# Two stores of layer 2 on ScalarE's DMA queue, and 16 buffers for the count blocks of the early products

## The chip, the cores and the metric

The kernel runs on one core of a Trainium2 chip. The metric is the device time of one execution, in microseconds (us); the time of a kernel is the median of several executions. A core has TensorE (PE), VectorE (DVE), ScalarE (ACT), GpSimd (POOL) and SyncE (SP). Each engine executes its own instructions in order, and SP, ACT and POOL each have a queue through which they issue DMA transfers. An instruction that waits for something holds all that is behind it on the same engine, DMA issues too.

## The reference

A graph network on 6250 nodes and 100,000 edges (sorted by destination): layer norm and ReLU, four SAGE layers of width 256 to 512, a final dense layer and a residual. Cut to what matters:

```
deg = segment_sum(ones, dst)
h1 = sage_mean(h0)                                   # 256 -> 512
hp = relu(h1 @ W2_pool + b2_pool)                    # layer 2: max pooling
hmax = where(deg > 0, segment_max(hp[src], dst), 0)
h2 = h1 @ W2_self + hmax @ W2_neigh + b2
h3 = ((segment_sum(h2[src], dst) + h2) / (deg + 1)) @ W3_neigh + b3
h4 = sage_mean(h3)
out = x + h4 @ W_fc + b_fc
```

The kernel merges weights across the layers: the products with `W3_neigh`, `W4_*` and `W_fc` are folded into the weights of layer 2, so that layer 2 gives rows that layer 3 only sums over the edges.

## The kernel before

**Tiles.** Nodes are cut into 49 tiles of 128, sorted edges into 782 tiles of 128. A sum over edges has two forms. For the destination tiles with many edges (0 to 15 for layer 3) it is a matrix product with a **count matrix** A: for each destination tile 49 blocks of 128 x 128 counts in fp8, made in the kernel and kept in DRAM as `tab_a` (784 KB for each of 18 tiles). For the others the source rows are gathered edge by edge. Rows that are summed later are kept to full precision as three bf16 parts (hi, mid, lo).

**Order of the work.** Layer 2 is one loop over the 782 edge tiles, in blocks and written out by hand; on each turn it advances several side works by a step each: the count matrices still to be made (`hub`), the early products (`early`) and the generators of finished node tiles (`now`). A scheduler then orders the instructions of each engine. In the profiled execution layer 2 lies at about 895 to 2330 us, its max pooling with what the change touches at about 1070 to 2330.

**The row flow.** Line L1354 (POOL) gathers 128 rows of 512 float32 values (256 KB) into X, which holds two such tiles; there are six X buffers (three each in two pools). L1335 (DVE) takes a running maximum over edges of one destination. L1339 (`stored`, SP) writes the rows to DRAM (`rows`). An X buffer is free for the next gather when DVE has read it and its store has landed. At the end of a block `carry` (L1197 to L1229) mends the first rows.

**done2 (L1243 on), once for each of the 49 node tiles.** `totals` gathers the maxima of the tile (L1235, POOL) and loads the first layer's tile th (L1241, through ACT's queue). PE transposes the maxima (L1254), ACT copies them (L1257), PE multiplies in float32 (L1261, L1264, L1267). Then the result is split: ACT casts hi (L1275), PE subtracts it (L1277), ACT casts mid (L1279), PE subtracts it (L1281), ACT casts lo (L1283), and **L1284 stores the three parts** `r3` (384 KB) to `tab_r`, through SP. Layer 3 reads `tab_r`.

**build_narrow (L356 on), for count matrices of the tiles 8 to 17.** ACT (L365, L372) and DVE (L367) make one-hot matrices, PE counts (L383), ACT copies the counts into A (L388), L398 checks them, and **L392 stores the finished matrix**, through SP. The tiles 0 to 7 are stored at L348, in another function, through SP as well.

**The early products.** While layer 2 still runs, the products of layer 3 for the count tiles 0 to 15 begin: as soon as four new row tiles are split (row tiles 37 down to 6), `early_products` adds 16 pieces of work. Each loads four count blocks (64 KB, L1311, SP) into a buffer `ae` (**L1310**), PE multiplies (L557, in `dense`), and the sum goes into `acc3` (L1125 on DVE, the first time L1128 on ACT). There are 128 such loads. The class `Hub` calls the load of a piece `LOOK` = 4 pieces ahead of its product, and `ae` has `LOOK + 3` = 7 buffers.

The parts of the code that the change touches:

Of the kernel before, what the change touches and what calls it, by code (L numbers as in the profile page):

```python
# [10 lines left out]
BF16 = mybir.dt.bfloat16  # L11
F16 = mybir.dt.float16
F8 = mybir.dt.float8e4
# [7 lines left out]
P = 128  # L21
# [57 lines left out]
def fast_path(  # L79
# [15 lines left out]
    nc = tc.nc  # L95
# [69 lines left out]
    tab_r = dram.tile([NP, 3 * FH], BF16, name="tab_r")  # L165
    tab_s = dram.tile([NP, 3 * FO], BF16, name="tab_s")
    tab_a = dram.tile([H4, P, NT, P // 2], BF16, name="tab_a")
# [79 lines left out]
    def bank(pool, tag, name, shape=None, bufs=None):  # L247
        t = pool.tile([P, FH], F32, tag=one_tag.get(id(pool), tag), name=name, **({"bufs": bufs} if bufs else {}))
        if shape is None:
            return t  # L250
        n = math.prod(shape)
        if len(shape) == 1:
            return t[:, :n]
        return t[:, :n].rearrange("p (a b) -> p a b", b=shape[1])
# [98 lines left out]
    def build_narrow(d, keys, pool, psb, copies):  # L353

        sk, mk, r0 = keys
        work = []  # L356
        held = {}
        for v in range(WT2):
            r = row_of[NW1 + (d - H1) * WT2 + v, 0] - r0

            def hot(r=r, v=v):
                i = v % 4
                if i == 0:
                    held["ht"] = pool.tile([P, 4, P], BF16, name="ht", bufs=2)
                nc.scalar.activation(held["ht"][:, i, :], iota_b, AF.Abs, bias=sk[:, r : r + 1])  # L365
                hm = pool.tile([P, NT * WIN2], BF16, name="hm", bufs=16)
                nc.vector.tensor_scalar(hm, iota_w[:, : NT * WIN2], mk[:, r : r + 1], None,  # L367
                                        op0=ALU.is_equal)
                held["hm", v] = hm
                if i == 3:  # L370
                    hs = pool.tile([P, 4, P], BF16, name="hs", bufs=5)
                    nc.scalar.activation(hs, held["ht"], AF.Relu, bias=one, scale=-1.0)  # L372
                    held["hs", v // 4] = hs

            def run(v=v):
                if v == 0:
                    held["A"] = pool.tile([P, NT, P], F8, name="A", bufs=2)
                A = held["A"]
                i = v % 2
                if i == 0:  # L380
                    held["pb"] = bank(psb, "pb", "pb", (2 * NT, WIN2))
                pb = held["pb"]
                nc.tensor.matmul(pb[:, i * NT : (i + 1) * NT, :].rearrange("p s c -> p (s c)"),  # L383
                                 held["hs", v // 4][:, v % 4, :], held.pop(("hm", v)),
                                 start=True, stop=True)
                def copy(pb=pb):
                    c = (v - 1) * WIN2
                    nc.scalar.copy(  # L388
                        A[:, :, c : c + 2 * WIN2].rearrange("p s (i c) -> p i s c", c=WIN2),
                        pb.rearrange("p (i s) c -> p i s c", s=NT), saturate=True)  # L390
                    if v == WT2 - 1:
                        nc.sync.dma_start(tab_a[d], A.bitcast(BF16))  # L392

                def look(n):
                    s0, s1 = LOOKS[n]
                    at = NW1 + len(LOOKS) * (d - H1) + n
                    many = pool.tile([P, 13, P], BF16, name="many", bufs=1)
                    nc.scalar.activation(many[:, : s1 - s0, :], A[:, s0:s1, :], AF.Relu,  # L398
                                         bias=less, accum_out=most[:, at : at + 1])

                if i == 1:
                    for f in copies[:2]:
                        f()
                    del copies[:2]
                    copies.insert(0, copy)
                    if v == WT2 - 1:
                        copies.extend(lambda n=n: look(n) for n in range(len(LOOKS)))

            work.append((hot, run))
        return work  # L410

    LOOK = 4
# [555 lines left out]
    with ExitStack() as on:  # L968
# [9 lines left out]
        def done1(d, acc):  # L978
# [31 lines left out]
            for k in range(KI):  # L1010
# [11 lines left out]
                        lambda acc, d=d: todo.append(done1(d, acc)), extra=3)  # L1022
# [107 lines left out]
    with tc.tile_pool(name="fl2c", bufs=1) as ck, ExitStack() as late:  # L1130
# [113 lines left out]
        def done2(d):  # L1244
            tots, th = totals(d)
            for _ in range(6):
                yield
            hm = tots[0]
            for t in tots[1:]:
                nc.vector.tensor_tensor(hm, hm, t, op=ALU.max)  # L1250
            yield
            pt = bank(pst, "pt", "pt_hTf", (KH, P))
            for j in range(KH):
                nc.tensor.transpose(pt[:, j, :], hm[:, j * P : (j + 1) * P], ident)  # L1254
            yield
            hT = wk.tile([P, KH, P], F32, name="hTf")
            nc.scalar.copy(hT, pt)  # L1257
            yield
            pm = bank(psm, "pm", "pm_prf")
            for k in range(KI):  # L1260
                nc.tensor.matmul(pm, th[:, k, :], usA[:, k, :], start=(k == 0), stop=False)  # L1261
            yield
            for k in range(KI):
                nc.tensor.matmul(pm, th[:, KI + k, :], usB[:, k, :], start=False, stop=False)  # L1264
            yield
            for c in range(KH):
                nc.tensor.matmul(pm, hT[:, c, :], un[:, c, :], start=False, stop=(c == KH - 1))  # L1267
                if c == 1:
                    yield
            yield  # L1270
            yield
            yield
            r3 = early_pool[0].tile([P, 3 * FH], BF16, name="r3", bufs=2 * BATCH + 1)
            hi, mid, lo = (r3[:, i * FH : (i + 1) * FH] for i in range(3))
            nc.scalar.copy(hi, pm)  # L1275
            yield
            nc.tensor.matmul(pm, minus_b, hi, start=False, stop=True, skip_group_check=True)  # L1277
            yield
            nc.scalar.copy(mid, pm)  # L1279
            yield  # L1280
            nc.tensor.matmul(pm, minus_b, mid, start=False, stop=True, skip_group_check=True)  # L1281
            yield
            nc.scalar.copy(lo, pm)  # L1283
            nc.sync.dma_start(tab_r[d * P : (d + 1) * P, :], r3)  # L1284
            if EARLY[0] <= d < EARLY[1]:
                ready.append((d, r3))
                if len(ready) == BATCH or d == EARLY[0]:
                    early_products()
            yield


        BATCH = 4
        ready = []
        early = Hub()
        early_pool = []
        summed = []

        def take_sums():
            while summed:
                add3(*summed.pop(0))  # L1300

        def early_products():
            batch = dict(ready)
            ss = sorted(batch)
            ready.clear()
            for d in range(H3):
                got = {}

                def load(d=d, got=got):
                    got[0] = early_pool[0].tile([P, BATCH, P], F8, name="ae", bufs=LOOK + 3)  # L1310
                    nc.sync.dma_start(got[0][:, : len(ss), :].bitcast(BF16),  # L1311
                                      tab_a[d, :, ss[0] : ss[-1] + 1, :])

                work = dense(ss, lambda s, got=got: got[0][:, s - ss[0], :],
                             lambda s: batch[s], FH, psd, lambda v, d=d: summed.append((d, v)),
                             own=d)

                def then(w):
                    take_sums()
                    w()  # L1320

                early.add([(load, work[0])] + [lambda w=w, i=i: then(w) if i == len(work) - 2 else w()
                                               for i, w in enumerate(work[1:])])
# [22 lines left out]
        for b in reversed(range(NB)):  # L1346
# [3 lines left out]
            for s0 in range(0, tb, G2):  # L1350
                X = (xmore if at // G2 % 2 else xpool).tile([P, G2, FH], F32, name="X2")
                for k in range(G2):
# [40 lines left out]
                    if (tiles and not ends and at >= begun_at + 11  # L1393
                            and begun2 < NT * (at - FIRST_AT) / (T - 20 - FIRST_AT)):
                        begun_at = at
                        now.append(done2(tiles.pop(0)))
                        begun2 += 1
# [10 lines left out]
        while tiles or now:  # L1408
            if tiles and len(now) < 2:
                now.append(done2(tiles.pop(0)))  # L1410
            for g in list(now):
                if next(g, 0) == 0:
                    now.remove(g)
# [42 lines left out]
    with ExitStack() as on:  # L1456
# [11 lines left out]
        with tc.tile_pool(name="fl3", bufs=2) as wk:  # L1468
# [36 lines left out]
            for d in range(H3):  # L1505
                work += dense([s for s0, s1 in late for s in range(s0, s1)], lambda s, d=d: block(d, s), lambda s: Z3[s], FH, psd,
                              lambda acc, d=d: todo.append(done3(d, acc)), own=d)
# [3 lines left out]
        with tc.tile_pool(name="fl4", bufs=2) as wk:  # L1511
# [22 lines left out]
            for d in range(H4):  # L1534
                parts4.append(dense([s for s0, s1 in order for s in range(s0, s1)],
                                    lambda s, d=d: block(d, s), lambda s: Z4[s], FO, psd,
                                    lambda acc, d=d: todo.append(done4(d, acc)), wide=True))
# [652 lines left out]
```

## Time and profile before

| | |
|---|---|
| time, median of 3 runs | 3315.81 us (3312.7 to 3325.22) |
| profiled execution | 3345.5 us, its span 3343.4 us |
| granted TensorE clock, mean | 0.895 of full speed |
| busy in the span | PE 75%, DVE 62%, POOL 58%, ACT 28% |
| DMA | 806.43 MB, mean 241 GB/s |
| DMAs of layer 2 through SP | 384 KB to `tab_r` x49; 256 KB rows; 64 KB `ae` x128; `tab_a` x18 (10 of them L392) |

The page of a profile shows one execution. A group of instructions has a name such as "L1284 SPq DMA_DIRECT2D tab_r<-r": the line of the kernel, the engine (SPq is SP's DMA queue, ACTq is ScalarE's), the operation, and what it writes and reads. A line of the waits, "SPq L1284 <- ACT r L1283: 141.4, 21, 16.9", says that the engine stood idle ahead of L1284 for 141.4 us in total, 21 times and at most 16.9 us, until the instruction after the arrow had ended. "remote" and "another core or an unknown queue" is a release whose source the profile could not name; "issue" is time in which the engine waited for nothing that the profile shows. The chain of waits goes back from the last instruction to what released it, and so on; its shares tell what the span is made of. Times are us from the start of the span.

### The profile page before, as it was taken

Reading aid. Unit: us, or ns where it says so; the run is one execution under the profiler, and the core shown is the slowest. Engines: PE = TensorE matmul, PEld = TensorE weight load, DVE = VectorE, ACT = ScalarE, POOL = GpSimd, SP = SyncE. Lnnn points to the kernel's source line nnn. Section 1 sums busy time; section 2 is a strip of 40 time slices with the busy share of each in tenths; the row PEclk is TensorE's granted clock in tenths of the full one; section 3 lists DMA queues with packets and bytes.
Section 4 is the critical chain, followed back from the end, with each engine's and each line's share of the span. In section 5 each row is a group of like instructions: output and inputs, shape, how many; then the busy total and the mean of one; then the engine's idle time right before and its main releaser. Section 6 shows DMA issues by size and latency. Waiting matters only on the chain.

```text
span 3343.4 us, 39175 instructions
## 1 busy us (share of the span) xinstructions
PE 2519.7 (75%) x11540; PEld 1299.7 (39%) x11671; DVE 2077.1 (62%) x5484; ACT 920.6 (28%) x2202; POOL 1939.8 (58%) x2260
## 2 busy tenths in 40 slices
PE   4367888889667463778578884876898888888887
PEld 2134555556443121333233432332333333444444
DVE  7766555555477866666667776664456666355555
ACT  4565555553266566411301011001000010000000
POOL 4456666666454656655556556653666665566664
PEclk9588999999888686889789997987999999999999
DMA  6545556666686878888788888875999998667675
GB/s 200 163 123 154 167 170 175 180 191 185 200 267 223 288 261 288 290 277 278 262 272 284 283 274 280 296 251 198 373 324 328 340 326 287 216 196 202 201 206 168
DMA packets 350539, 806.43 MB, mean 241 GB/s; under 512 B 55806, under 2 KB 147430, under 8 KB 350284
## 3 DMA queue, kind: packets, MB, share of 16 engines
q0 software_dynamic: 146160, 514.05, 49.5%
q1 hardware_dynamic: 146072, 234.34, 19.3%
q10 hardware_dynamic: 58084, 55.44, 5.5%
q8 instruction: 94, 1.54, 0.2%
q14 instruction: 129, 1.06, 0.1%
HBM read 605.25 MB, written 199.17 MB: 241 GB/s over the span
## 4 chain that ended last, share of the span: by engine, by line
PE 56%; issue 15%; DVE 10%; DMA 8%; another core or an unknown queue 6%; ACT 4%; POOL 1%; ACTq 0%; SPq 0%; DVEq 0%; POOLq 0%
PE pd L557 15%; PE pg L498 10%; PE pd L549 5%; DVE run L1335 3%; PE pd L550 3%; PE pm_hp L1008 3%; PE pm_prf L1267 3%; PE pm_hp L1011 3%; PE pm_w L269 2%; PE pb L339 2%; PE pg L493 2%; DMA X<-rows,srcIf 2%; PE pm_prf L1261 2%; DVE X L1335 2%
## 5 line engine op out<-in xcount | busy, mean ns | idle before, releaser
L1354 POOL DMA_INDIRECT X<-rows,srcIf x782 | 744.1, 952 | 548.5 <-issue 218.1
L1335 DVE SCALAR_TENSOR_TENSOR run<-run,samef,X 128x512 f32<-128x512 f32 x758 | 572.6, 755 | 90.1 <-DMA X<-rows,srcIf 69.1
L476 POOL DMA_INDIRECT ring<-tab_h,srcT x474 | 455.3, 961 | 287.0 <-issue 97.3
L498 PE MATMUL pg<-ring,hot 128*128 128x259 bf16 (+1 forms) x2432 | 528.7, 326 | 81.5 <-issue 38.2
L527 DVE SCALAR_TENSOR_TENSOR acc<-pg,M,acc 128x256 f32<-128x256 f32 (+2 forms) x694 | 356.5, 538 | 176.7 <-PE pg L498 64.3
L557 PE MATMUL pd<-r,ae 128*128 128x512 bf16 x1494 | 396.0, 405 | 78.3 <-issue 36.3
L476 POOL DMA_INDIRECT ring<-tab_r,srcE x342 | 332.2, 971 | 189.6 <-issue 76.9
L476 POOL DMA_INDIRECT ring<-tab_s,srcE x314 | 301.9, 962 | 189.7 <-issue 70.0
L498 PEld LDWEIGHTS <-hot 128*128 128x128 bf16 x2448 | 243.5, 100 | 315.6 <-issue 167.0
L472 DVE TENSOR_SCALAR hot<-iota_bf,keyE 128x128 bf16<-128x128 bf16 x656 | 159.5, 270 | 262.8 <-PE pg L494 103.1
L549 PE MATMUL pd<-zt,ac 128*128 128x512 bf16 x835 | 298.2, 386 | 30.1 <-issue 24.4
L1335 DVE SCALAR_TENSOR_TENSOR X<-X,samef,run 128x512 f32<-128x512 f32 x379 | 281.6, 743 | 49.8 <-issue 22.6
L557 PEld LDWEIGHTS <-ae 128*128 128x128 fp8e4 x1536 | 158.2, 103 | 362.5 <-issue 233.9
L550 PE MATMUL pd<-zt,ac 128*128 128x256 bf16 x882 | 244.3, 277 | 27.0 <-issue 23.2
L557 PE MATMUL pd<-zt,ac 128*128 128x512 bf16 x797 | 227.1, 381 | 16.2 <-issue 14.5
L557 PE MATMUL pd<-Z,A 128*128 128x256 bf16 (+1 forms) x1176 | 196.4, 281 | 30.0 <-issue 16.1
L339 PE MATMUL pb<-hm,hs 128*128 128x392 bf16 x461 | 156.3, 362 | 76.5 <-DVE hm L333 45.2
L331 ACT ACTIVATE hs<-ht,onef 128x128 bf16<-128x128 bf16 x423 | 161.8, 393 | 185.4 <-PE pb L339 82.2
L472 DVE TENSOR_SCALAR hot<-iota_bf,keyT 128x128 bf16<-128x128 bf16 x474 | 121.4, 267 | 126.6 <-PE pg L498 51.7
L1267 PE MATMUL pm_prf<-unf,hTf 128*128 128x512 f32 x392 | 187.4, 603 | 9.2 <-issue 8.4
L333 DVE TENSOR_SCALAR hm<-iota_w,mk 128x392 bf16<-128x392 f16 x461 | 153.3, 345 | 53.8 <-remote 15.3
L1125 DVE TENSOR_TENSOR acc<-acc,pd 128x512 f32<-128x512 f32 x112 | 76.4, 683 | 150.4 <-remote 105.3
(342 smaller groups left out, 3597.6 us busy)
## 6 DMA issues: line engine op xcount, KB each, us to landing
rows<-X SPq DMA_DIRECT2D x385, 256.0 KB
tab_r<-r SPq DMA_DIRECT2D x49, 384.0 KB
tab_a<-A SPq DMA_DIRECT2D x18, 784.0 KB
tab_t<-th SPq DMA_DIRECT2D x49, 256.0 KB
rows<-hpf SPq DMA_DIRECT2D x49, 256.0 KB
th<-tab_t ACTq DMA_DIRECT2D x49, 256.0 KB
X<-rows,srcIf POOLq DMA_INDIRECT x782
ac<-tab_a ACTq DMA_DIRECT2D x90, 112.0 KB
```

Of the source, the lines that this page charges most:

```text
L331: nc.scalar.activation(hots[0], t, AF.Relu, bias=one, scale=-1.0)
L339: nc.tensor.matmul(hold[0], hots[0], hots[1], start=(k == 0), stop=(k == k_of[w] - 1))
L472: nc.vector.tensor_scalar(hot[j], iota_b, keyT[:, j - jb : j - jb + 1], None, op0=ALU.is_equal)
L476: nc.gpsimd.indirect_dma_start(out=ring[:, j % deep, :], out_offset=None, in_=table, in_offset=bass.IndirectOffsetOnAxis(ap=srcT[:, j - jb ...
L498: nc.tensor.matmul(pg[:, : F + c], hot[j], X[:, part * F : (part + 1) * F + c], start=(k == 0 and part == 2), stop=(k == n - 1 and part == 1),
L527: nc.vector.scalar_tensor_tensor(acc[d], half, m, acc[d], op0=ALU.mult, op1=ALU.add)
L549: nc.tensor.matmul(hold[0], a, z[:, : 2 * F], start=(s == ss[0]), stop=False)
L550: nc.tensor.matmul(hold[0][:, :F], a, z[:, 2 * F :], start=False, stop=(s == ss[-1]))
L557: nc.tensor.matmul(hold[0][:, : F + c], a, z[:, part * F : (part + 1) * F + c], start=(s == ss[0] and part == 2 and s != own), stop=(s == ...
L1267: nc.tensor.matmul(pm, hT[:, c, :], un[:, c, :], start=False, stop=(c == KH - 1))
L1335: nc.vector.scalar_tensor_tensor(put, held, st, row, op0=ALU.mult, op1=ALU.max)
L1354: nc.gpsimd.indirect_dma_start(out=X[:, k, :], out_offset=None, in_=tab_p, in_offset=bass.IndirectOffsetOnAxis(ap=srcI[:, t : t + 1], axis=0),
```

## The change

Three edits. The store of a finished count matrix in `build_narrow` and the store of the split rows in `done2` are issued through ScalarE's queue, right behind the ScalarE instruction that writes the last of their data. The buffers of the count blocks of the early products become 16 instead of 7.

```diff
@@ build_narrow.run.copy, L392
                     if v == WT2 - 1:
-                        nc.sync.dma_start(tab_a[d], A.bitcast(BF16))
+                        nc.scalar.dma_start(tab_a[d], A.bitcast(BF16))
@@ done2, L1284
             nc.scalar.copy(lo, pm)
-            nc.sync.dma_start(tab_r[d * P : (d + 1) * P, :], r3)
+            nc.scalar.dma_start(tab_r[d * P : (d + 1) * P, :], r3)
@@ early_products.load, L1310
-                    got[0] = early_pool[0].tile([P, BATCH, P], F8, name="ae", bufs=LOOK + 3)
+                    got[0] = early_pool[0].tile([P, BATCH, P], F8, name="ae", bufs=16)
                     nc.sync.dma_start(got[0][:, : len(ss), :].bitcast(BF16),
                                       tab_a[d, :, ss[0] : ss[-1] + 1, :])
```

On SP the order of the instructions that remain is the same, but for the loads of L1311: nine more of them stand ahead of the first product, and later each stands ahead of a product nine pieces further on. On the other engines the order changes in small places only (57 on PE, 77 on DVE, 43 on ACT, 9 on POOL).

## The prediction

> **What bounds the kernel now.** I read the page first (span, busy shares), then the table by stretches of layer 2, where everything that the change touches lies (about 1070 to 2330 us), then the chain of waits there, then the waits of SP and of GpSimd (POOL), and last the timelines at one place. The stretches (columns: PE, weight loads, DVE, ACT, POOL busy, granted clock, DMA share, GB/s):
>
> ```profile
> 1070.00:1200.00 130.00, 67.75 (x206) 27.64 (x205) 103.08 (x284) 79.43 (x180) 74.88 (x78) 0.71 0.78 260
> 1200.00:1400.00 200.00, 101.94 (x288) 42.95 (x288) 140.48 (x302) 115.10 (x263) 116.40 (x124) 0.72 0.83 281
> ...
> 1800.00:2000.00 200.00, 168.06 (x595) 75.30 (x606) 151.81 (x219) 19.19 (x33) 116.57 (x124) 0.93 0.86 282
> ```
>
> Until 1400 PE is half busy and DVE the busiest (141 of 200); after 1400, when the early products run, PE is at 168 of 200. So two flows share the stage. The **row flow**: POOL gathers X, DVE takes the running maximum, SP stores the rows, and the store frees X for the next gather. The **PE flow**: early products and the second layer's outputs. The chain of waits over the two parts, first 1070 to 1400, then 1400 to 2330:
>
> ```profile
> by line: issue 21.0%; DVE run L1335 11.8%; DMA X<-rows,srcIf 11.2%; DVE X L1335 7.1%; another core or an unknown queue 7.0%; DVE hm L367 5.1%; PE pm_prf L1261 3.5%; PE pm_prf L1267 3.2%; ACT ht L365 3.0%; ACT A L388 2.6%; DMA rows<-X 2.5%;
> ```
>
> ```profile
> by line: PE pd L557 24.1%; issue 20.8%; another core or an unknown queue 13.2%; PE pm_prf L1267 8.3%; DVE run L1335 7.5%; PE pm_prf L1261 4.8%; PE pm_prf L1264 4.8%; DMA zt<-tab_r 4.5%; DVE X L1335 3.4%; DMA X<-rows,srcIf 2.3%; DMA rows<-X
> ```
>
> I weigh the flows by these shares. Before 1400 the row flow has 11.8 + 11.2 + 7.1 + 2.5 = 32.6 and PE 3.5 + 3.2 = 6.7, so 0.83 of the two. After 1400 the rows have 7.5 + 3.4 + 2.3 + 2.0 (18.4 of 930 us are the row store there) = 15.2, PE 24.1 + 8.3 + 4.8 + 4.8 = 42.0: 0.27. What a faster row flow is worth is its gain times these shares; that is a choice of mine, and the two ends (all of it, none of it) are rivals below.
>
> SP issues in order. What it waited for between 1070 and 2330 (us in total, times, longest):
>
> ```profile
> SPq L1339 <- DVE X L1335: 188.5, 111, 11.2
> SPq L1284 <- ACT r L1283: 141.4, 21, 16.9
> SPq L1311 <- remote: 136.2, 24, 13.6
> SPq L1311 <- PE pd L557: 53.0, 29, 8.4
> ...
> SPq L392 <- ACT A L388: 6.9, 3, 3.2
> ```
>
> So SP stood 141.4 us ahead of the store of the split rows (L1284), with finished row stores (L1339) queued behind. That hurts only where POOL waits for such a store:
>
> ```profile
> POOL X L1354 <- issue: 194.4, 558, 2.7
> POOL X L1354 <- DVE run L1335: 69.5, 40, 7.2
> POOL X L1354 <- DMA rows<-X: 61.0, 31, 7.9
> ```
>
> One place shows it, SP first, then POOL (start, us, what, idle before):
>
> ```profile
> 1162.32 2.33 SPq L1339 DMA_DIRECT2D rows<-X  x3
> 1179.28 0.32 SPq L1284 DMA_DIRECT2D tab_r<-r  x1
> 1179.69 1.59 SPq L1339 DMA_DIRECT2D rows<-X  x3
> ```
>
> ```profile
> 1174.82 0.95 POOL L1354 DMA_INDIRECT X<-rows,srcIf  x1 [0.30 <-issue]
> 1183.05 0.95 POOL L1354 DMA_INDIRECT X<-rows,srcIf  x1 [7.28 <-DMA rows<-X]
> ```
>
> SP held three stores for 14.6 us (1164.65 to 1179.28), until ScalarE's last cast (L1283) was done; the gather at 1183.05 lost 7.28 us.
>
> **Part 1, the stores leave SP.** From SP go 49 issues (L1284) and 10 (L392) with their waits; its other instructions keep their order, except the loads of part 3. I replayed SP's row stores from 1070 on: each is ready when the DVE instruction that writes its rows ends, SP's other waits stay where they were measured, and those two lines are struck out. The stores' summed time from ready to issue falls from 605 to 201 us. Most of that is worth nothing, as six X buffers cover it. Where a gather waited for the row store, its gain is the smaller of its wait and of the store's head start: 30.4 us of the 61.0, 13.1 of them before 1400 (7.3 at 1183, then 2.5, 1.1, 2.1 and crumbs) and 17.3 after (3.0, 2.9, 3.2, 7.5 and crumbs). The rest of the 61.0 stays: it is the landing itself (3.8 us median from issue) and SP's 189.2 us at the loads (L1311). With the shares: 13.1 x 0.83 + 17.3 x 0.27 = 10.9 + 4.7 = **15.6 us gained**. Late next, at the same gathers: DVE's running maximum (69.5 and 52.4 us of POOL's waits already).
>
> A rule of the Trainium skill speaks against this. "DMA: Bandwidth & Descriptors", section "Issuing engines are not separate DMA queues", says that DMAs started by any engine run on the same 16 DMA engines, and that starting them from several engines saves only the issuing time. By it the sum of part 1 would be 59 issues off SP, which is on no path here, so 0 us. The trace does not contradict the engines being shared, but the wait of 141.4 us in SP's queue is no issuing time, and the page does not speak of it.
>
> **Part 2, the stores arrive on ScalarE.** Each sits right behind the instruction that makes its data (L1283, L388), so its data wait is about that instruction's own 0.59 or 0.50 us. The trace has this very kind of issue on ACT's queue:
>
> ```profile
> L1241 ACTq DMA_DIRECT2D th<-tab_t x49: 326/326/444, 1064.4 to 2229.6; - x49
> ```
>
> 59 x 0.326 = 19.2 us of ACT. Behind a store wait the next casts, copies (L1257) and count work (L365, L372), and PE waits for those. All of it on the path: 19.2 us; none: 0. In the chain up to 1400 ACT's pieces are about 35 of 330 us, 11%; after it ACT is 19 of 200 us busy and not among the lines printed. I take 11%: **2.1 us lost**. A wait at issue for an earlier transfer that shares the store's completion semaphore: in the run before, the transfers that would be those predecessors were issued 6.7 to 38 us ahead of the store, against 3.2 to 4.7 us that such transfers need to land. So 0; the other end is the one wait of SP for a landing (2.6 us, at L1453) at each of the 11 stores of L1284 before 1400, where ACT is busy: 29 us. I take 0, since the 49 th loads issue on this queue in 0.444 us at most.
>
> **Part 3, sixteen count blocks.** PE's weight loads stand 0.12 to 0.28 us before the first use of almost every block, and blocks are issued 20 to 96 us ahead (the first seven 350): PE does not wait for blocks, so earlier blocks gain 0 directly. Could SP's 189.2 us (136.2 + 53.0) at L1311 go? Those are loads that wait for a buffer. In the changed order nine more loads go ahead at the start, and each load then waits for the product 16 blocks back, not 7. But the load that waits for a given product stands behind the same row store as before, so SP stops there as before. So 0 again; the end on the good side is POOL's waits for stores held by L1311, 22 us by the same replay. On the bad side, six of the early loads now stand one or two row stores behind the place of L392 and need that count matrix landed, 4.7 us (its median) after its issue: at most 6 x 4.7 = 28 us of SP, in place of the 6.9 us of L392. In the run before, 38 us of stores' delay came from L392 and cost POOL nothing. I take 0.
>
> **Sum.** 15.6 - 2.1 = 13.5 us. Profiled execution: 3345.5 (span 3343.4), so 3332.0. That execution is 29.7 us (0.9%) above the median of the runs, 3315.81; the saving is taken off as it is: **3302 us**, -0.4%. About 0.5% (16.6 us) is what a measurement of this kernel can tell from no change, so "faster" is below 3299.2, "slower" above 3332.4.
>
> **Rivals.**
> 1. All of the 30.4 us comes through: 3285. It asks that the PE flow after 1400 be paced by the rows too (its products are released step by step with the gathers in program order). For: "issue" and the row lines are a third of that chain. Against: PE at 168 of 200. With row stores that also land sooner, no longer behind 384 KB in one queue, some us more: 3275 to 3297.
> 2. Nothing comes through: 3316. POOL's waits on stores turn into waits on DVE or on X landing, as the DMA engines are 0.78 to 0.87 busy either way. For: DVE's waits at POOL are twice the size of the store's. Against: at 1183 DVE had no part in the 7.28 us. 3311 to 3321. The rule of the Trainium skill ends at this time too.
> 3. Slower: ScalarE becomes the place that is held. It issues in order, and the store stands between the casts and copies that PE needs (PE already waits 67.6 us at L1277 for L1275). If all 59 issues lie on the path and the rows give nothing: 3315.8 + 19.2 = 3335. If, besides, th loads land later behind 384 KB stores in ACT's queue (L1275 waited four times for th; 4 x 3.9 us, a store's landing) 3351. With the rows' gain as I have it, the issues outweigh it once 15.6 / 19.2 = 0.81 of them lie on the path; with no gain from the rows, the time is above 3332.4 from 16.6 / 19.2 = 0.86 on.
> 4. The sixteen buffers free SP after all (22 us more, 3280), or do nothing; the forecast has them do nothing.
>
> **How the numbers follow.** Forecast, 3294 to 3311: 0.42, of which 0.10 is below 3299. Rivals 1 and 4 together: 0.25, all faster. Rival 2: 0.11, all within. Rival 3: 0.22, of which 0.20 above 3332. So faster 0.35, same 0.45, slower 0.20. Leaving out about a tenth at each end, the range is 3273 (just under the low end of rival 1) to 3337 (just over the 3335 of rival 3).
>
> **What would show it.** Right: SP's waits at L1284 and L392 gone; POOL's wait on row stores from 61 to about 30 us in 1070 to 2330; SP's waits at L1311 near 189; a stage shorter before 1400 by about 10 us, afterwards by about 5; ACT issues of some 0.33 us, no waits of several us ahead of them. Wrong: POOL's waits move to DVE or X one for one (rival 2); waits at L1284 appear on ACT, or PE's wait at L1277 or L1261 grows (rival 3); L1311's waits shrink (rival 4); a part of the gain outside layer 2 would be none of my steps.

## The result and the profile after

The changed kernel takes **3297.81 us**, median of 15 runs (3277.05 to 3311.55), beside 3315.84 us for the kernel before, median of 15 (3287.79 to 3335.68): 18.0 us less, ratio 0.995, 95% interval 0.9926 to 0.9973. A second set gave 3298.51 beside 3316.69 us, ratio 0.9944 (0.9914 to 0.9974). The forecast was 3302 us, 13.5 us less. At -0.54% it lies just over the 0.5% that the prediction called what a measurement can tell. The ratios leave out runs over 1.5% above the fastest of their kernel, which in two of the later sets takes out 4 of 35 runs of the kernel before and none of the others, so a ratio need not be the quotient of the medians.

The profiled execution took 3277.05 us, its span 3275.1. Against the one of before that is 68 us, nearly four times the difference of the medians: the profiled execution of before lies above all 15 runs beside it, and this one is the fastest of its 15. Of two single profiles one may read where waits stand, and hardly how long a stage is.

SP's waits after the change, 1070 to 2330 us (total, times, longest):

```profile
SPq L1339 <- DVE X L1335: 252.2, 126, 12.1
SPq L1311 <- remote: 131.2, 21, 13.6
SPq L1311 <- PE pd L557: 52.6, 28, 4.2
...
SPq L1311 <- DMA tab_a<-A: 9.9, 2, 5.6
```

L1284 and L392 are gone from the list. The loads of count blocks still hold SP as long as before (remote and PE pd together: 183.8 after 189.2 us). The first line has grown, and that is harmless: SP waits there for rows that do not exist yet. Finished rows wait for SP far less. By the replay's own measure, row stores stand ready for 184 us in total before they are issued, after 605 (forecast: 201; 235 in the second profile of the same kernel). POOL's waits in the same stretch:

```profile
POOL X L1354 <- issue: 194.5, 553, 2.4
POOL X L1354 <- DVE X L1335: 65.0, 35, 8.2
POOL X L1354 <- DVE run L1335: 51.2, 32, 6.6
POOL X L1354 <- DMA rows<-X: 33.2, 28, 8.4
```

The wait for row stores fell from 61.0 to 33.2 us (30.0 in the second profile); the forecast was "about 30". The two DVE lines together stay where they were (121.9, now 116.2; 125.3 in the second profile). The stores on ScalarE's queue (duration min/median/max in ns):

```profile
L1284 ACTq EVENT_SEMAPHORE  x49: 17/17/17, 1139.7 to 2263.8; - x49
L1284 ACTq DMA_DIRECT2D tab_r<-r x49: 326/326/362, 1141.5 to 2264.1; - x49
```

An issue lasts 326 ns in the median, as the th loads had said, and the step before it, where it would wait for an earlier transfer, always 17 ns. ScalarE does wait elsewhere for these stores to land, 23.1 us in five waits and 16.7 in four in the second profile, where it had none before; but its waits for th fell from 43.7 us to 15.3 and 20.7. PE's wait at L1277 for L1275, the sign of a held ScalarE, did not grow clearly (67.6, now 70.5 and 33.7). The stretches that answer to those of before:

```profile
1070.00:1200.00 130.00, 69.87 (x200) 29.65 (x201) 99.85 (x244) 77.49 (x173) 80.32 (x85) 0.68 0.87 288
1200.00:1400.00 200.00, 124.52 (x356) 56.61 (x356) 144.57 (x297) 108.34 (x247) 129.07 (x136) 0.80 0.91 312
...
1800.00:2000.00 200.00, 146.69 (x555) 65.70 (x554) 150.73 (x229) 24.39 (x39) 119.81 (x126) 0.86 0.87 285
```

POOL issues more gathers in the same time up to 1400 (85 + 136 instructions after 78 + 124). Which hundred us hold which work has shifted, so I also compare by gather number, further below.

### The profile page after: what moved, and what is told of

Read it like the earlier page. It is cut to its first block, busy times and chain, and to the rows that moved or that the text cites. A ratio compares the mean times of both kernels' runs of the same rounds, so it can differ in the third digit from the quotient of the medians.

```text
span 3275.1 us, 39283 instructions
## 1 busy us (share of the span) xinstructions
PE 2517.3 (77%) x11671; PEld 1304.7 (40%) x11671; DVE 2075.2 (63%) x5484; ACT 917.6 (28%) x2202; POOL 1940.9 (59%) x2260
## 4 chain that ended last, share of the span: by engine, by line
PE 56%; issue 13%; DVE 11%; DMA 6%; another core or an unknown queue 6%; ACT 5%; POOL 2%; SPq 0%; ACTq 0%; DVEq 0%; POOLq 0%
PE pd L557 14%; PE pg L498 11%; PE pd L549 6%; DVE run L1335 4%; PE pd L550 3%; PE pm_hp L1008 3%; PE pm_w L269 3%; PE pm_hp L1011 3%; PE pm_prf L1267 2%; PE pb L339 2%; PE pg L493 2%; PE pm_prf L1261 2%; DVE X L1335 2%; PE pm_prf L1264 1%
## 5 line engine op out<-in xcount | busy, mean ns | idle before, releaser
L527 DVE SCALAR_TENSOR_TENSOR acc<-pg,M,acc 128x256 f32<-128x256 f32 (+2 forms) x694 | 356.2, 538 | 160.3 <-PE pg L498 55.1
L557 PE MATMUL pd<-r,ae 128*128 128x512 bf16 x1536 | 387.5, 394 | 43.4 <-DVE acc L1125 22.8
L549 PE MATMUL pd<-zt,ac 128*128 128x512 bf16 x882 | 317.2, 390 | 28.1 <-issue 22.8
L557 PE MATMUL pd<-zt,ac 128*128 128x512 bf16 x816 | 228.0, 379 | 16.2 <-issue 15.7
L557 PE MATMUL pd<-Z,A 128*128 128x256 bf16 (+1 forms) x1176 | 194.6, 280 | 22.8 <-issue 10.9
L1267 PE MATMUL pm_prf<-unf,hTf 128*128 128x512 f32 x392 | 195.4, 626 | 7.9 <-issue 5.2
L1125 DVE TENSOR_TENSOR acc<-acc,pd 128x512 f32<-128x512 f32 x112 | 76.3, 681 | 141.4 <-remote 99.2
```

The lines of the kernel that those rows point to most:

```text
L527: nc.vector.scalar_tensor_tensor(acc[d], half, m, acc[d], op0=ALU.mult, op1=ALU.add)
L549: nc.tensor.matmul(hold[0], a, z[:, : 2 * F], start=(s == ss[0]), stop=False)
L557: nc.tensor.matmul(hold[0][:, : F + c], a, z[:, part * F : (part + 1) * F + c], start=(s == ss[0] and part == 2 and s != own), stop=(s == ...
```

## The experiments

Each ratio is to the kernel before on the same chip. A difference of medians stands beside it. A single part of this change is smaller than most of these intervals, so where the time leaves a question open the waits in the traces answer it, or it stays open.

**One part alone.** Four kernels on one chip, before 3312.92 us.

The split rows alone:

```diff
-            nc.sync.dma_start(tab_r[d * P : (d + 1) * P, :], r3)
+            nc.scalar.dma_start(tab_r[d * P : (d + 1) * P, :], r3)
```

> Only the split-row stores (L1284) go to ScalarE's queue; L392 stays on SP and the count blocks keep 7 buffers. Theory A (row stores were held behind L1284 on SP, and POOL waited for them): nearly the whole gain is here, ratio to the kernel before about 0.995 (0.992 to 0.998), SP's wait at L1284 gone, POOL's wait on row stores from 61 to about 32 us. Rival B (the gain comes from the sixteen buffers or from L392): ratio 0.999 to 1.001. Rival C (ScalarE's issues cost about as much as SP gains): 0.999 to 1.003.

The count matrices alone:

```diff
-                        nc.sync.dma_start(tab_a[d], A.bitcast(BF16))
+                        nc.scalar.dma_start(tab_a[d], A.bitcast(BF16))
```

> Only the count-matrix stores of build_narrow (L392) go to ScalarE's queue. Theory A: ratio 0.999 to 1.001, since the 38 us of delay that L392 caused to row stores cost POOL nothing; POOL's wait on row stores stays near 61 us. Rival B (the stores of 784 KB held SP's queue or row landings where it mattered): 0.996 to 0.998.

The buffers alone:

```diff
-                    got[0] = early_pool[0].tile([P, BATCH, P], F8, name="ae", bufs=LOOK + 3)
+                    got[0] = early_pool[0].tile([P, BATCH, P], F8, name="ae", bufs=16)
```

> Only the buffers of the count blocks become 16; every engine but SP has the same order as before. Theory A: ratio 0.999 to 1.002, SP's waits at L1311 near 189 us as before, or a little more where an early load waits for tab_a to land (at most 28 us on SP). Rival B (the buffers free SP): 0.993 to 0.997 and waits at L1311 well under 150 us.

Both stores with 7 buffers (the first two edits together):

> Both stores on ScalarE's queue, the count blocks with 7 buffers: the change without its third part. Theory A: ratio as of the whole change, 0.995 (0.992 to 0.998), the buffers being worth nothing. Rival B (buffers do it): 0.998 to 1.001. If early loads behind tab_a cost something, this one is a little faster than the whole change, 0.992 to 0.994.

| kernel | median us | against before | ratio, 95% interval | POOL waits for row stores, us |
|---|---|---|---|---|
| L1284 alone | 3307.14 | -5.8 | 1.0001 (0.9968 to 1.0035) | 55.1 |
| L392 alone | 3305.27 | -7.7 | 0.9986 (0.9956 to 1.0016) | 38.1 |
| 16 buffers alone | 3311.73 | -1.2 | 1.0013 (0.9974 to 1.0051) | 57.1 |
| both stores | 3300.94 | -12.0 | 0.9973 (0.9936 to 1.001) | 15.1 |

None of the four intervals leaves out 1, so by time alone no part is shown to gain, the two stores together come nearest, and the buffers show nothing. Of the rest I had expected nearly all at L1284 and nothing at L392, and that is not what came: L1284 alone shows no gain. Its one trace suggests why. SP's waits with L1284 alone moved, 1070 to 2330:

```profile
SPq L1339 <- DVE X L1335: 241.2, 130, 13.4
SPq L1311 <- remote: 171.3, 29, 14.8
SPq L1311 <- PE pd L557: 74.6, 36, 16.3
SPq L392 <- ACT A L388: 30.2, 5, 13.4
SPq L1339 <- DMA tab_r<-r: 29.1, 4, 10.8
```

The 141.4 us ahead of L1284 are gone, and SP stands at the next things in its queue. At L392 it waits 30.2 us for the counts (and 10.3 us, a line further down, for L365) instead of 6.9. At L1311 it waits 245.9 instead of 189.2. In 29.1 us that before did not have, a row store waited for the landing of a split-row store: the transfers of SP and ScalarE take turns on the same eight completion semaphores, and in these four waits the last user of the row store's semaphore was a split-row store from ScalarE. Together 33.6 + 56.7 + 29.1 = 119.4 us of new waits stand against the 141.4 that went. POOL's wait for row stores is hardly shorter:

```profile
POOL X L1354 <- DMA rows<-X: 55.1, 25, 13.6
```

Between 1070 and 1440, where L392 is mostly active, it is 28.1 us here and 20.5 in the kernel before. Once L392 goes too, it does not come among the seven longest waits of POOL in that stretch.

The 119.4 us are not all lost, though. Row stores stand ready but not issued for 364 us with L1284 alone, after 605 before, and for 127 with both stores moved (519 with L392 alone, 669 with the buffers alone). And the longer waits at L1311 belong to this run: with both stores moved they are 179.4 us, as before. Moving one store also changes the order of the other engines' work in places, and that was not tested apart from the queue.

L392 alone did more than I had expected as well:

```profile
SPq L1284 <- ACT r L1283: 107.8, 18, 17.0
POOL X L1354 <- DMA rows<-X: 38.1, 31, 7.9
```

POOL's wait for row stores fell by 23 us with L1284 still on SP, where I had expected it to stay near 61.

**Thinner and thicker cover.** The number of X buffers, five or seven in place of six, in both kernels. With five, PE, DVE, ACT and SP of the kernel before keep their order:

```diff
-        xmore = late.enter_context(tc.tile_pool(name="xrows2", bufs=3))
+        xmore = late.enter_context(tc.tile_pool(name="xrows2", bufs=2))
```

> The kernel before with five X buffers in place of six (the second pool of X has two). PE, DVE, ACT and SP have the same order as before; only the cover that lets a row store be late is thinner. Theory A (late row stores reach the end through POOL's wait for a free X): clearly slower than before, ratio 1.006 to 1.02, POOL's wait on row stores far over 63 us. Rival B (POOL's waits are made up for by other flows, and the change's gain comes from the new order of the instructions): within 0.997 to 1.004.

> The changed kernel with five X buffers. Theory A: with thin cover the two moved stores matter more, so this is faster than the kernel before with five buffers by more than the 17 us of the change at six: by 25 to 45 us; ratio to the kernel before 0.995 to 1.005. Rival B: the same 10 to 18 us below its partner as at six buffers.

Seven:

```diff
-        xmore = late.enter_context(tc.tile_pool(name="xrows2", bufs=3))
+        xmore = late.enter_context(tc.tile_pool(name="xrows2", bufs=4))
...
-                seg = wk.tile([P, P + 1], F32, name="segf", bufs=2)
+                seg = wk.tile([P, P + 1], F32, name="segf", bufs=1)
```

> The kernel before with seven X buffers (the second pool four; the scan rows of carry one buffer instead of two to make room; DVE's order changes in places). Theory A: more cover does part of what the change does, ratio 0.994 to 0.998, POOL's wait on row stores under 40 us with both stores still on SP. Rival B: 0.999 to 1.003.

> The changed kernel with seven X buffers. Theory A: little is left to cover, so 0 to 6 us below the change, ratio to the kernel before 0.992 to 0.996. Rival D (DVE or the DMA engines bound the row flow by now): equal to the change, 0.994 to 0.996, with POOL's waits on DVE grown by what the waits on stores lose.

These ran on a chip where the kernel before takes 2800.47 us.

| kernel | median us | ratio, 95% interval |
|---|---|---|
| before, 5 X buffers | 2980.08 | 1.0648 (1.0633 to 1.0663) |
| changed, 5 | 2983.61 | 1.0653 (1.0638 to 1.0667) |
| before, 7 | 2798.40 | 1.0 (0.9985 to 1.0015) |
| changed, 7 | 2789.80 | 0.9962 (0.9949 to 0.9975) |

Two expectations of my theory failed, and a third had its size wrong. A sixth buffer is worth 180 us, where I had expected 17 to 56, so cover decides; but with five the change gives nothing, and a seventh gives the kernel before nothing. With five, POOL's waits 900 to 2060, before, then 900 to 2070, changed (the three longest ahead of a gather, without "issue"):

```profile
POOL X L1354 <- DVE run L1335: 93.2, 95, 3.1
POOL X L1354 <- DMA rows<-X: 63.3, 57, 5.9
POOL X L1354 <- DVE X L1335: 49.6, 45, 4.9
```

```profile
POOL X L1354 <- DVE run L1335: 99.2, 100, 5.0
POOL X L1354 <- DVE X L1335: 68.0, 46, 4.6
POOL X L1354 <- DMA rows<-X: 48.7, 49, 3.6
```

What the row stores lose, 14.6 us, the running maximum takes and more (6.0 + 18.4; other DVE lines lose 11.6). That reads like rival 2, but there was hardly anything to move: on this chip row stores stand ready before their issue for only 22 us in total with five buffers, with the change and without, where the first profile had 605. So at most 22 of POOL's 63.3 us there can come from SP. The wait ahead of L1284 is small from the start, too: 17.6 us with five buffers and 46.9 with seven, beside 141.4 in the first profile (19.1 and 26.6 ahead of L392, beside 6.9). So the five buffers hardly test the theory. With seven buffers the change still gives 8.6 us. Where they come from is not shown: the stores' time from ready to issue falls from 65 to 38 us, POOL's wait for them from 23.1 to 19.6, and the time from gather 100 to the last gather is the same in the one profile of each (975.7 and 975.4 us). The change alone, with six, was not run on that chip.

**The stores stay on SP, only later.** The test of the queue against two other causes: the new order of the other engines' instructions, and the second hardware queue. Both stores are kept in a list and issued on SP behind a later row store; PE, DVE and ACT keep the order of before.

```diff
-            nc.sync.dma_start(tab_r[d * P : (d + 1) * P, :], r3)
+            owed.append([4, tab_r[d * P : (d + 1) * P, :], r3])
...
-                        nc.sync.dma_start(tab_a[d], A.bitcast(BF16))
+                        owed.append([3, tab_a[d], A.bitcast(BF16)])
...
+        def pay(row, n=1):
+            for o in list(owed):
+                o[0] -= n
+                if o[0] <= 0:
+                    owed.remove(o)
+                    with tc.issue_after(row.ins): nc.sync.dma_start(o[1], o[2])
```

> The kernel before, with both stores still on SP but behind later row stores: L1284 four row stores after the place where its data is due by the program, L392 three. PE, DVE and ACT have exactly the order of before, and ScalarE issues nothing more. Theory A (SP stood in order behind data that was not ready, and row stores behind it): the gain of the change or most of it, ratio 0.994 to 0.997 where before takes about 3313 us, with SP's waits at these stores nearly gone. Rival B (the new order of the other engines, or a second hardware queue for the 384 KB stores, gives the gain): 0.999 to 1.002. On a chip where before takes about 2800 us the row flow waits on transfers instead, and A expects 0.996 to 0.999.

> The changed kernel beside the others on one chip. Where before takes about 3313 us: 0.9926 to 0.9973. Where before takes about 2800 us: theory A 0.995 to 0.999 (less POOL wait for stores to win there); a theory that the gain is a fixed count of instructions would give 17 us of 2800, 0.994.

And SP's last long waits, those at L1311, taken away as well: the load is issued behind the row store ahead of it in the program, first in the changed kernel, then in the one with later stores.

```diff
-                    nc.sync.dma_start(got[0][:, : len(ss), :].bitcast(BF16),
-                                      tab_a[d, :, ss[0] : ss[-1] + 1, :])
+                    with tc.issue_after(last_row[0].ins): nc.sync.dma_start(
+                        got[0][:, : len(ss), :].bitcast(BF16), tab_a[d, :, ss[0] : ss[-1] + 1, :])
```

> The changed kernel, and each load of count blocks (L1311) is issued behind the row store ahead of it in the program, about four pieces ahead of its product, not as soon as its buffer falls free. Theory A: SP's 184 us of waits at L1311 go as well, and with them the rest of POOL's waits on row stores: 5 to 20 us below the change. Rival B (that cover is off the path, PE paces the second half): equal to the change within 4 us. If loads come late for PE instead: slower than the change, with waits of L557 for ae.

> The kernel before with both stores later on SP as in the first of these runs, 16 buffers, and the loads of count blocks behind the row stores as in the third: no transfer leaves SP, ScalarE issues nothing more. Theory A: as the third run within 5 us, or 2 us less for ScalarE's 59 issues. Rival C (ScalarE's issues cost what they last, 19 us): 10 us or more below the third.

| kernel | median us | against 3316.69 | ratio, 95% interval | POOL waits for row stores, us |
|---|---|---|---|---|
| stores later on SP | 3303.35 | -13.3 | 0.9987 (0.9954 to 1.002) | 35.8 |
| the change | 3298.51 | -18.2 | 0.9944 (0.9914 to 0.9974) | 30.0 |
| the change, loads later | 3316.21 | -0.5 | 1.0014 (0.998 to 1.0048) | 19.1 |
| all later on SP | 3310.71 | -6.0 | 0.9998 (0.9966 to 1.0031) | 22.2 |

With the stores later on SP (their issue is line L1296 there):

```profile
SPq L1296 <- DMA th<-tab_t: 11.6, 1, 11.6
SPq L1296 <- ACT r L1283: 4.4, 2, 4.0
POOL X L1354 <- DMA rows<-X: 35.8, 23, 8.1
```

SP's waits at them are down to 16.6 us (11.6 + 4.4 + 0.4 + 0.2), POOL's wait for row stores is nearly as in the changed kernel, and the median is 13.3 us lower. The ratio, 0.9987, lies just below the rival's 0.999 to 1.002 and above the 0.994 to 0.997 that I had expected, and its interval reaches into both, so the time decides nothing here. For POOL's waits the traces, one or two of each kernel, do: SP's order makes them, and neither the reordering of the other engines nor ScalarE's queue is needed for that. That the 18 us come from these waits is argued from this, and not shown by a time.

The loads put later were meant to win more, and lost the whole gain. SP hardly waits at L1311 any more, and row stores stand ready for only 146 us, less than in the change. But other engines now wait for L1311 (who waited, us, times, over the whole execution):

```profile
  ACT r L1275: 57.9, 2
  PEld L557: 22.2, 10
  PE pd L557: 17.0, 7
```

PE's two lines, which overlap, are loads that come too late for their product; in the kernel before no wait of PE is put down to L1311. The ACT line is no such proof, since L1275 reads no count block. More is lost in one place (1070 to 2330):

```profile
DVE hm L367 <- PE pb L383: 47.0, 4, 44.3
POOL X L1354 <- DVE hm L367: 55.3, 20, 40.6
```

One wait of 44.3 us, until 1571, holds VectorE at the count work for PE's product L383, which stood behind early products, and a gather waits 40.6 us with it. With all stores and loads later on SP the longest wait of this kind is 32.7 us, in the change 12.3. So a shorter wait for row stores is not by itself a shorter time, and early loads that look free can be worth their 184 us of SP's time. How much of the loss comes from late loads, and how much from the new order of PE that this edit brings, was not separated. The kernel with all of it on SP is 5.5 us below the one with ScalarE's 59 issues, just over the 5 that I had expected at most and well short of the 10 or more that would speak for a price of the issues.

## Why the prediction held, step by step

- **SP's hold and its reach (part 1): right.** Waits at L1284 and L392 gone, row stores ready before their issue for 184 us (forecast 201), POOL's wait on them 33.2 and 30.0 us (about 30).
- **The share that reaches the end: right in kind, low in size.** I took 15.6 of 30.4 us as reaching the end and 2.1 us as lost; 18.0 and 18.2 us were measured, with an interval of about 9 to 25. The weights by the chain's shares were a choice; with the 2.1 us put back, 20.1 of 30.4 would be 0.66 instead of 0.51. All of it (rival 1, 3285) did not come, though the upper end of rival 1's range, 3297, is about 1 us from the medians; nor did nothing (rival 2, 3316). That the total came this close is in part luck, as the next points show.
- **Where it lies: only roughly.** I gave 10.9 us to the time before 1400 and 4.7 to the rest. By gather number, which stands for the same work in every profile (us from gather 100 to 300, and from 300 to the last):

| profile | 100 to 300 | 300 to 781 |
|---|---|---|
| before | 360.2 | 841.2 |
| 16 buffers alone | 368.3 | 838.2 |
| L1284 alone | 368.5 | 828.6 |
| L392 alone | 355.7 | 837.8 |
| stores later on SP | 358.7 | 818.1 |
| both stores | 344.8 | 821.7 |
| the change | 335.9 | 822.4 |
| the change, second profile | 355.6 | 834.7 |

  Both stores on SP in their old place: 364.3 and 839.7 on average; both on ScalarE: 345.4 and 826.3. So both stretches gain, 19 and 13 us in these few profiles, more in all than the medians do; two profiles of the changed kernel itself differ by 20 and 12. The second stretch gains more than the 4.7 us that I gave it. L1284 alone is shorter only in the second stretch, L392 alone mainly in the first, where six of its ten stores are issued. That would fit L392 holding SP in the first stretch once L1284 is gone, but these are single profiles. Ahead of gather 100 and behind the last gather the two groups overlap (1074.5 and 1086.9 us beside 1067.2 to 1077.4; 1041.5 and 1055.2 beside 1046.2 to 1050.6), so no gain outside is seen.
- **ScalarE's issues (part 2): the duration right, the loss not visible.** 326 ns each. The kernel that issues nothing more on ScalarE is not faster than the change (3303.35 beside 3298.51), so nothing shows the 19.2 us of rival 3 on the path. The landing waits that I took as 0 came elsewhere: on SP, for a transfer of ScalarE's queue, 29.1 us in the run with L1284 alone and 7.3 us (for th) in the changed kernel; and on ScalarE, 23.1 and 16.7 us for its own stores, away from the issue. So the 0 was too low as a wait, though the total shows nothing of it.
- **Sixteen buffers (part 3): right in the result.** 1.0013 alone, and L1311's waits as long as before. My bound for early loads that wait for a count matrix, 28 us of SP, was too low: 9.9 us in one profile of the changed kernel and 44.9 in the other, while POOL's wait on row stores was 33.2 and 30.0.
- **What failed: L392.** The step was "38 us of stores' delay came from L392 and cost POOL nothing". With L1284 gone, SP stood at L392 for 40.5 us. And with L392 alone gone, POOL's wait for row stores fell from 61.0 to 38.1 us, so even beside L1284 it was not free in that profile. In the sum I had struck out both at once, so the total stood; the reading that one store carries the gain did not.
- **Rival 4 (the buffers free SP): refuted** by the buffers alone. By the rule of the Trainium skill ("DMA: Bandwidth & Descriptors", "Issuing engines are not separate DMA queues"), as the prediction applied it, there would have been no gain; the measured 18 us are more than that. As argued above they come from the waiting ahead of an issue, of which the page does not speak. Moving the stores within one engine's queue lowers the median by 13.3 us, with an interval of the ratio that reaches past 1.

Open stay the split between the two stores (-5.8 and -7.7 us in the medians, while both ratios' intervals hold 1), a proof in time that the order of SP alone gives the gain, and what the change is worth with six buffers on the chip of 2800 us.

## What to carry to other kernels

An instruction that waits in an in-order queue of DMA issues can cost what stands finished behind it, and only where someone waits for that; both can be read off the trace before anything is moved. Strike out all the blockers of a queue in one replay, not one at a time: with one gone, the queue can run up to the next. Here the wait at L392 went from 6.9 to 40.5 us, and with one store moved row stores still stood ready for 364 us, with both for 127. A wait that looks free, as that of the early loads, may be the lead that another engine lives on.

## What the runs showed that I had not expected

One kernel, two speeds: on two chips before took 3312.92 and 3316.69 us, on a third 2800.47, 15% less. The engines work alike: a running maximum lasts 755 ns in the profile of before and in that of the kernel with seven buffers on the third chip, a gather's issue 952 and 953. The transfers differ. The kernel with seven buffers on the third chip, in the stretch after gather 300 (columns as in the stretches above):

```profile
1200.00:1880.00 680.00, 593.46 (x2265) 274.03 (x2264) 594.25 (x911) 110.11 (x202) 494.35 (x521) 0.94 0.98 341
```

The same work took 841 us in the first profile of the kernel before, which has six buffers (on the third chip a seventh made no difference: 2798.40 beside 2800.47), at a DMA share of 0.83 and 273 GB/s:

```profile
1447.00:2288.00 841.00, 631.46 (x2228) 284.27 (x2269) 588.75 (x899) 111.58 (x203) 490.87 (x517) 0.87 0.83 273
```

On the third chip the DMA engines are busy nearly all the time (0.98); in the first profile they are less busy (0.83), though the time is longer. What makes the difference between the chips was not tried.
